# Layer 0 of a decoder: statistics of four chunks together, and gated integers quantised in two halves from a copied scale row

## The chip, the cores and the metric

The kernel runs on one core of a Trainium2 chip. The metric is device time in microseconds, from one launch, lower is better. A core has five engines that run their own instruction queues in order and wait for each other by semaphores: TensorE (PE in the profile; its weight loads are PEld), VectorE (DVE), ScalarE (ACT), GpSimd (POOL) and SyncE (SP, which here only issues DMAs).

## The reference

Two decoder layers over x of 4 batches x 1024 tokens x 256 channels in float32, each layer with self attention, cross attention to a context of 154 tokens, and a feed forward, each followed by x = layernorm(x + f(x)). Layer 0's feed forward is the part that matters most here, a pair of "bit linear" layers with integer activations and ternary weights:

```python
def act_quant(x):
    scale = 127.0 / jnp.clip(jnp.max(jnp.abs(x), axis=-1, keepdims=True), 1e-05)
    return jnp.clip(jnp.round(x * scale), -128, 127) / scale
...
h = bit_linear(x, w1)                 # 256 -> 1024
h = depthwise_conv1d(h.transpose(0, 2, 1), conv_w, conv_b)
h = h.transpose(0, 2, 1)
h = jax.nn.silu(h)
return bit_linear(h, w2)              # 1024 -> 256
```

The gated hidden values (after silu) need one scale per token: 127 over the largest of a token's 1024 absolute values. They are multiplied by it, rounded to integers, and go into the second product. The cross attention of layer 0 has 16 heads of 64, and its output, plus x, is normalised.

## The kernel before, in words

**Tiling.** x lies in SBUF for the whole run, one tile per batch: 128 partitions (tokens) x 8 chunks x 256 channels. Products go through 128 x 128 weight loads and write PSUM banks of 512 floats.

**Stages.** Layer 0's self attention comes first (until about 690 us). Then one list of events holds three things: layer 0's cross attention, layer 0's feed forward, and layer 1's self attention. Feed forward of batches 0 and 1 runs beside cross attention of later batches; feed forward of batches 2 and 3 runs beside layer 1's self attention. Layer 1's cross attention and feed forward close the kernel.

**Order.** Every piece of work is a Python function put into the list with a time in units of its own. `run_in_order` sorts by time (ties keep the order of insertion) and calls them. Instructions on PE, and the last steps of a layernorm, are pinned to that order (`tc.keep_in_program_order`). On the other engines a scheduler orders the instructions beforehand: when an engine is free by its plan, it takes the oldest instruction that is ready, so that work of a later event can run earlier where an engine would stand idle. The feed forward's `schedule` rounds every time before unit 135 down to a whole unit plus 0.42, which places these events in the gaps of the cross attention's own.

**Cross attention, layer 0** (`wide_cross_attention`). A step s is one of 32 (batch, half of the tokens, group of four heads); it takes four units. After each half's last step, `out_projected` (line 775) runs four times, once a chunk: eight products (L574 through the helper `mm`), an add into x (L781) and `measured` (lines 130 to 137), which takes the mean and variance of a chunk with two VectorE instructions, L136 and L137. After the fourth it calls `layernorm`, which forms the reciprocal roots on POOL (L154) and puts the scaling of x (L169) off by six events.

**Feed forward, layer 0** (`feed_forward`). Per batch: `token_scales` (L844), `quantised_x` (a mult L852 and a rounding L858 per half), `token_rows`. Then four rounds r of 256 tokens, in which hidden channels lie on partitions: the tile gt holds 128 x 8 x 256 floats, of which there is one buffer. In a round, `hidden` and `gated` run four times each (products, convolution L920 and L924, gate L934, largest absolute value L939 to L944). Then:

- `hidden_scales`: two PE transposes of the maxima (L949), a reduce (L951) and the four small instructions of `act_scales` (L833, L835, L836, L838) that give the scale sc and its inverse;
- `quantised_hidden`: two PE transposes (L957) spread sc over all partitions as a row in a PSUM bank, one VectorE product of gt with that row (L961), one rounding to bf16 integers into gq (L964);
- `fed_forward`: sixteen products of gq with the second weight (L574), then x is updated (L976) and normalised.

The times within a round, as shares of the batch's length: `hidden_scales` at u + 16 (15.5 for batches 2 and 3), `quantised_hidden` at u + 18.5, `fed_forward` at u + 23, next round at u + 21. A batch has 38, 38, 39 and 40 units. The tile tagged "xq" (one buffer) is shared by the quantised x and the running maximum am of `gated`.

Of the kernel before, what the change touches and what calls it, by code (L numbers as in the profile page):

```python
# [8 lines left out]
F32 = mybir.dt.float32  # L9
BF16 = mybir.dt.bfloat16  # L10
U8 = mybir.dt.uint8
AF = mybir.ActivationFunctionType
ALU = mybir.AluOpType
# [3 lines left out]
P = 128  # L17
# [8 lines left out]
RND = 12582912.0  # L26
# [3 lines left out]
def decoder_kernel(ctx: ExitStack, tc: tile.TileContext, a: dict, out: bass.AP):  # L30
    nc = tc.nc
# [99 lines left out]
    def measured(b, c):  # L131

        if c % 4 == 0:
            measures[b, c // 4] = small.tile([P, 4, nc.vector.BN_AGGR_DIM], F32, tag="bnmv", name="bnmv", bufs=6)
        st = small.tile([P, nc.vector.BN_STATS_DIM], F32, tag="bnst", name="bnst", bufs=2)
        nc.vector.bn_stats(st, xs[b][:, c, :])  # L136
        nc.vector.bn_aggr(measures[b, c // 4][:, c % 4, :], st)  # L137

    def layernorm(b, c0, n, scalar=False, then=None, wait=6):


        xb = xs[b][:, c0 : c0 + n, :]
        if n == 4:
            mv = measures.pop((b, c0 // 4))
        else:
            st = small.tile([P, 2, nc.vector.BN_STATS_DIM], F32, tag="bnst2", name="bnst2", bufs=2)
            mv = small.tile([P, 2, nc.vector.BN_AGGR_DIM], F32, tag="bnmv2", name="bnmv2", bufs=3)
            for c in range(n):
                nc.vector.bn_stats(st[:, c, :], xb[:, c, :])
                nc.vector.bn_aggr(mv[:, c, :], st[:, c, :])  # L150
        ve = small.tile([P, 4], F32, tag="ve", name="ve", bufs=2)
        nc.vector.tensor_scalar(ve[:, :n], mv[:, :n, 1], EPS, None, ALU.add)  # L152
        rstd = small.tile([P, 4], F32, tag="rstd", name="rstd", bufs=3)
        nc.gpsimd.tensor_tensor(rstd[:, :n], ve[:, :n], neghalf[:, :n], ALU.pow)  # L154

        def last_step():
            pin = tc.keep_in_program_order
            if scalar:
                nmr = small.tile([P, 4], F32, tag="nmr", name="nmr", bufs=2)
                pin(nc.vector.scalar_tensor_tensor(  # L160
                    nmr[:, :n], mv[:, :n, 0], -1.0, rstd[:, :n], ALU.mult, ALU.mult
                ))
            for c in range(n):
                if scalar:
                    pin(nc.scalar.activation(
                        xb[:, c, :], xb[:, c, :], AF.Identity, bias=nmr[:, c : c + 1], scale=rstd[:, c : c + 1]
                    ))
                else:
                    pin(nc.vector.tensor_scalar(  # L169
                        xb[:, c, :], xb[:, c, :], mv[:, c, 0:1], rstd[:, c : c + 1], ALU.subtract, ALU.mult  # L170
                    ))
            if then:
                then()

        pending.append([wait, b, last_step, c0])
# [394 lines left out]
    def pe(ins):  # L570
        tc.keep_in_program_order(ins)

    def mm(o, l, r, start, stop):
        pe(nc.tensor.matmul(o, l, r, start=start, stop=stop))  # L574
# [3 lines left out]
    def at(when, f, *args):  # L578
        events.append((when, len(events), f, args))
# [15 lines left out]
    def wide_cross_attention(wk, wf, slot, bank):  # L595
# [179 lines left out]
        def out_projected(b, qh, k):  # L775
            t = bank()
            c = 4 * qh + k
            for t8 in range(8):
                ot = ots[8 * b + 4 * qh + t8 // 2, t8 % 2]
                mm(t[:, :E], ot[:, k * P : (k + 1) * P], l0x_wo[:, t8, :], t8 == 0, t8 == 7)  # L780
            nc.vector.tensor_tensor(xs[b][:, c, :], t[:, :E], xs[b][:, c, :], ALU.add)  # L781
            measured(b, c)
            if k == 3:
                layernorm(b, 4 * qh, 4)


# [17 lines left out]
        for s in range(8 * NB):  # L804
            for j in range(4):
                at(4 * s + j, scores, s, j)
                at(4 * s + j + 3.4, turned, s, j)
            for i in range(2):
                at(4 * s - 3.4 + 2 * i, queries, s, i)
                at(4 * s + 7.9 + 2 * i, weighted, s, i)  # L810
            if s % 4 == 3:
                for k in range(4):
                    last = s == 8 * NB - 1
                    at(4 * s + (10.7 + k if last else (13.45, 17.45, 21.45, 23.45)[k]), out_projected, s // 8, s // 4 % 2, k)


    def feed_forward(wf, bank):
# [7 lines left out]
        scs, dqs, xqTs, rows, edges, gts, ams, sc2s, dq2s, gqs, ths = ({} for _ in range(11))  # L825
        Q = 4
        N = S // Q
# [123 lines left out]
            nc.vector.tensor_reduce(amax, t[:, :N].rearrange("p (j n) -> p j n", j=2), AX.X, ALU.max)  # L951
            sc2s[b, r], dq2s[b, r] = act_scales(amax, w2m)

        def quantised_hidden(b, r):
            t = bank()
            for j in range(2):
                pe(nc.tensor.transpose(  # L957
                    t[:, j * P : (j + 1) * P], sc2s[b, r][:, j : j + 1].to_broadcast([P, P]), ident
                ))
            g = gts[b, r]  # L960
            nc.vector.tensor_tensor(g, g, t[:, :N].unsqueeze(1).to_broadcast([P, 8, N]), ALU.mult)  # L961

            gqs[b, r] = wf.tile([P, 8, N], BF16, tag="gq", name="gq", bufs=1)
            nc.vector.tensor_scalar(gqs[b, r], g, RND, RND, ALU.add, ALU.subtract)  # L964

        def fed_forward(b, r):
            t = bank()
# [13 lines left out]
        def schedule(b, t0, length, start):  # L981
            def on(share, f, *args):
                when = t0 + length * share / 100.0

                at(int(when) + 0.42 if when < start - 4 else when, f, b, *args)

            inside = t0 + length < start
            on(0, token_scales)
            for q in range(2):
                on(3 + 2 * q, quantised_x, q)  # L990
                on(5.5 + 2 * q, token_rows, q)
            on(9, edge_tokens)
            for r in range(Q):
                u = 11 + 21 * r
                for m in range(4):
                    d = 2.65 if inside else 2.0
                    on(u + d * m, hidden, r, m)
                    on(u + d * (m + 1.5), gated, r, m)
                on(u + (16 if inside else 15.5), hidden_scales, r)
                on(u + 18.5, quantised_hidden, r)  # L1000
                on(u + 23, fed_forward, r)

        return schedule
# [115 lines left out]
    wf = ff_stack.enter_context(tc.tile_pool(name="ffn", bufs=1, side="right", reuse_waits="tile"))  # L1119
# [518 lines left out]
```

## Time and profile before

| | us |
|---|---|
| median of the 3 runs shown | 2301.23 |
| their lowest and highest | 2296.64, 2302.22 |
| the profiled execution: its time | 2297.67 |
| the profiled execution: its span (first to last instruction) | 2295.9 |
| granted TensorE clock, mean over the span | 0.977 |

| busy over the span | us | share |
|---|---|---|
| PE | 2158.2 | 94% |
| DVE | 1495.3 | 65% |
| ACT | 1130.5 | 49% |
| POOL | 507.7 | 22% |

| lines that the change touches | instructions | mean ns |
|---|---|---|
| L136, chunk statistics, 128x256 (whole kernel) | 160 | 420 |
| L137, their combination (whole kernel) | 160 | 174 |
| L957, transposes of the scales | 32 | 285 |
| L961, product of gt and the row, 128x2048 | 16 | 2280 |
| L964, rounding into gq, 128x2048 | 16 | 1228 |

How to read it: a row of instructions has the line, the engine, the operation, the tiles it writes and reads, how often, and busy time. A row of waits has who waited, for whom, and then total us, times and the longest. A timeline row has the start and duration in us, and in brackets the idle time of the engine before it with what ended it. A busy engine is not an engine at its peak, and an average over the span mixes stages with different limits.

### The profile page before, as it was taken

How to read it: one execution, taken by the hardware profiler on the slowest of the kernel's cores; microseconds unless marked ns; L12 is line 12 of the kernel's file. 1: busy time of each engine (PE TensorE's matmuls, PEld its weight loads, DVE VectorE, ACT ScalarE, POOL GpSimd, SP SyncE). 2: the span in 40 equal slices, each digit the busy share in tenths (PEclk: the TensorE clock that was granted, in tenths of full speed). 3: DMA queues.
4: the chain of work that ended last, by engine and by line, in shares of the span. 5: the costliest groups of instructions: out<-in, count | busy, mean ns of one | idle time of the engine just before them, and what ended most of it. 6: DMA issues, size and time to landing. Idle time of an engine off the chain costs nothing.

```text
span 2295.9 us, 38089 instructions
## 1 busy us (share of the span) xinstructions
PE 2158.2 (94%) x14196; PEld 1271.0 (55%) x14228; DVE 1495.3 (65%) x3287; ACT 1130.5 (49%) x2925; POOL 507.7 (22%) x1113
## 2 busy tenths in 40 slices
PE   7999999999999899999999998889989999999996
PEld 4444454455444456656556555656666755565554
DVE  4665666667666556557997887785883365555644
ACT  1455555554555365555665655444542334535443
POOL 1111111111112265444444443000000021111102
PEclk8999999999999999999999999999999999999998
DMA  3101110000000100000000000000000010010101
GB/s 89 40 22 33 33 29 15 10 15 15 6 15 1 38 1 19 1 1 1 1 1 1 33 1 22 0 1 1 1 1 1 1 20 15 10 30 14 28 1 37
DMA packets 24440, 34.78 MB, mean 15 GB/s; under 512 B 5952, under 2 KB 19648, under 8 KB 24256
## 3 DMA queue, kind: packets, MB, share of 16 engines
q1 hardware_dynamic: 22640, 31.20, 5.9%
q8 instruction: 113, 1.85, 0.3%
q10 hardware_dynamic: 1616, 1.16, 0.2%
q14 instruction: 71, 0.58, 0.1%
HBM read 15.56 MB, written 4.19 MB: 9 GB/s over the span
## 4 chain that ended last, share of the span: by engine, by line
PE 71%; DVE 19%; ACT 6%; issue 1%; POOL 1%; DMA 1%; SPq 0%; ACTq 0%; POOLq 0%; DVEq 0%
PE s L191 21%; PE t L574 15%; PE s L1174 10%; PE s L574 9%; PE acc L191 6%; DVE gt L924 3%; PE acc L1174 3%; DVE nmp L332 2%; PE t L758 2%; ACT u L733 2%; DVE x L169 1%; DVE nmx L729 1%; DVE bnst L136 1%; PE t L1082 1%; DVE ht L910 1%
## 5 line engine op out<-in xcount | busy, mean ns | idle before, releaser
L398 ACT ACTIVATE p<-s 128x512 f32<-128x512 f32 (+1 forms) x640 | 320.5, 554 | 286.1 <-PE s L191 283.7
L332 DVE TENSOR_REDUCE nmp<-s 128x1 f32<-128x512 f32 (+3 forms) x640 | 298.0, 522 | 154.2 <-PE s L191 153.9
L191 PE MATMUL s<-qs,kp 32*128 32x512 f32 (+3 forms) x1536 | 369.2, 525 | 5.3 <-DVE nmp L332 5.3
L191 PE MATMUL s<-kp,qp 32*128 32x128 f32 (+3 forms) x2304 | 327.5, 408 | 2.1 <-DMA qp<-sq 1.9
L741 POOL TENSOR_SCALAR p<-u,rs 128x128 f32<-128x128 f32 x512 | 214.6, 437 | 294.5 <-DVE rs L737 203.1
L191 PEld LDWEIGHTS s<-kp,qp 32*128 32x128 f32 x2304 | 166.9, 189 | 142.9 <-ACT p L398 45.1
L401 POOL TENSOR_SCALAR_AFFINE_SELECT p<-p 128x256 f32<-128x256 f32 x256 | 101.1, 410 | 640.0 <-ACT p L398 639.7
L733 ACT ACTIVATE u<-s,nmx 128x154 f32<-128x154 f32 x512 | 192.0, 388 | 31.6 <-DVE nmx L729 27.9
L191 PEld LDWEIGHTS s<-qs,kp 32*128 32x128 f32 x1536 | 144.2, 184 | 62.0 <-DVE nmp L332 29.2
L154 POOL TENSOR_TENSOR rstd<-ve,neghalf 128x4 f32<-128x4 f32 (+1 forms) x56 | 55.1, 984 | 545.5 <-DVE ve L152 541.4
L191 PE MATMUL acc<-p,v 128*32 128x512 f32 (+3 forms) x1536 | 159.8, 496 | 1.2 <-ACT ot L440 0.8
L574 PEld LDWEIGHTS s<-kt,qt 64*128 64x128 f32 x1024 | 103.1, 189 | 71.8 <-issue 53.3
L574 PE MATMUL s<-kt,qt 64*128 64x154 f32 x1024 | 137.1, 317 | 0.5 <-ACT qt L715 0.3
L574 PE MATMUL t<-xT,xw 128*128 128x512 f32 x256 | 124.2, 608 | 10.4 <-DVE xT L661 6.6
L729 DVE TENSOR_REDUCE nmx<-s 128x4 f32<-128x616 f32 x128 | 101.2, 791 | 49.9 <-PE s L574 49.7
L1331 DVE TENSOR_REDUCE nmt<-s 128x3 f32<-128x462 f32 (+1 forms) x192 | 99.0, 578 | 45.2 <-PE s L1174 45.1
L924 DVE SCALAR_TENSOR_TENSOR gt<-ht,cw,gt 128x256 f32<-128x256 f32 x256 | 117.5, 498 | 6.6 <-ACT gt L920 5.5
L574 PE MATMUL t<-xw,ot 128*128 128x256 f32 x512 | 116.3, 381 | 3.6 <-ACT pr L762 1.7
L574 PE MATMUL t<-v,pt 128*128 128x256 f32 x512 | 116.2, 380 | 3.1 <-DVE pt L1083 3.1
L574 PE MATMUL s<-qt,xT 128*128 128x512 f32 x256 | 118.4, 606 | 0.0
L348 DVE TENSOR_REDUCE nmp<-s 128x4 f32<-128x512 f32 x128 | 82.5, 687 | 48.6 <-PE s L191 41.3
L574 PEld LDWEIGHTS t<-v,pt 128*128 128x128 f32 x512 | 96.0, 190 | 23.3 <-issue 6.0
(259 smaller groups left out, 3896.2 us busy)
## 6 DMA issues: line engine op xcount, KB each, us to landing
qp<-sq SPq DMA_DIRECT2D x128, 64.0 KB, 2.4
kp<-sk SPq DMA_DIRECT2D x64, 64.0 KB, 2.3
out_dram<-x SPq DMA_DIRECT2D x8, 512.0 KB, 2.9
x<-in_x_dram SPq DMA_DIRECT2D x3, 1024.0 KB, 5.5
wf<-in_L_ffn_w_dram SPq DMA_DIRECT2D x2, 1024.0 KB, 6.0
xw<-in_L_xattn_wk_dram SPq DMA_DIRECT2D x1, 1024.0 KB, 5.2
xw<-in_L_xattn_wq_dram SPq DMA_DIRECT2D x1, 1024.0 KB, 5.7
xw<-in_L_xattn_wv_dram SPq DMA_DIRECT2D x1, 1024.0 KB, 5.2
```

The lines of the kernel that those rows point to most:

```text
L191: pe(nc.tensor.matmul(o, l, r, start=start, stop=stop))
L332: nc.vector.tensor_reduce(nmp[:, 2 * pair + g, qc, i : i + 1], t[g][:, c0 : c0 + n], AX.X, ALU.max)
L348: nc.vector.tensor_reduce(nmp[:, 2 * pair + g, q0 : q0 + 4, 0], t[g].rearrange("p (j n) -> p j n", j=4), AX.X, ALU.max,)
L398: nc.scalar.activation(p[:, g, :total], t[g][:, :total], AF.Exp)
L401: nc.gpsimd.affine_select(out=v, in_=v, compare_op=ALU.is_ge, fill=0.0, base=0, pattern=[[0, 2], [1, P]], channel_multiplier=-1,)
L574: pe(nc.tensor.matmul(o, l, r, start=start, stop=stop))
L729: nc.vector.tensor_reduce(nmx.rearrange("p i g -> p g i"), t, AX.X, ALU.max, negate=True)
L733: nc.scalar.activation(u[:, 2 * i + g, :], t[:, g, i, :], AF.Exp, bias=nmx[:, i, g : g + 1], accum_out=ssum[:, i, g : g + 1],)
L741: nc.gpsimd.tensor_scalar(p[:, h * P : (h + 1) * P], u[:, h, :P], rs[:, h : h + 1], 1.0, ALU.mult, ALU.mult)
L924: nc.vector.scalar_tensor_tensor(g, ht[:, i, k : k + N], cw[:, hc, k : k + 1], g, ALU.mult, ALU.add)
L1174: pe(nc.tensor.matmul(o, l, r, start=start, stop=stop))
L1331: nc.vector.tensor_reduce(nmts[s % 2][:, 3 * u : 3 * u + n, g, 17], ts[g][:, : n * LK].rearrange("p (c k) -> p c k", k=LK), AX.X, ALU.max, ...
```

## The change

In cross attention, the statistics of the four chunks of a half are taken together, after the fourth chunk's add. In the feed forward, the transposes that spread sc become an event of their own, `hidden_rows`, at u + 17.2, and ScalarE copies the row from PSUM into an SBUF tile (tag "xq", in the place of am, which is no longer needed by then). `quantised_hidden` runs twice, at u + 18.5 and u + 20, on four of the eight channel blocks each: a product of half of gt with the row in SBUF, and a rounding into half of gq.

```diff
             nc.vector.tensor_tensor(xs[b][:, c, :], t[:, :E], xs[b][:, c, :], ALU.add)
-            measured(b, c)
             if k == 3:
+                for c in range(4 * qh, 4 * qh + 4):
+                    measured(b, c)
                 layernorm(b, 4 * qh, 4)
...
-        def quantised_hidden(b, r):
+        def hidden_rows(b, r):
             t = bank()
             for j in range(2):
                 pe(nc.tensor.transpose(
                     t[:, j * P : (j + 1) * P], sc2s[b, r][:, j : j + 1].to_broadcast([P, P]), ident
                 ))
-            g = gts[b, r]
-            nc.vector.tensor_tensor(g, g, t[:, :N].unsqueeze(1).to_broadcast([P, 8, N]), ALU.mult)
-
-            gqs[b, r] = wf.tile([P, 8, N], BF16, tag="gq", name="gq", bufs=1)
-            nc.vector.tensor_scalar(gqs[b, r], g, RND, RND, ALU.add, ALU.subtract)
+            row = ams[b, r] = wf.tile([P, 2, N], F32, tag="xq", name="row", bufs=1)
+            nc.scalar.copy(row[:, 0, :], t[:, :N])
+
+        def quantised_hidden(b, r, i):
+            if i == 0:
+                gqs[b, r] = wf.tile([P, 8, N], BF16, tag="gq", name="gq", bufs=1)
+            part = slice(4 * i, 4 * i + 4)
+            g = gts[b, r][:, part, :]
+            nc.vector.tensor_tensor(g, g, ams[b, r][:, 0, :].unsqueeze(1).to_broadcast([P, 4, N]), ALU.mult)
+
+            nc.vector.tensor_scalar(gqs[b, r][:, part, :], g, RND, RND, ALU.add, ALU.subtract)
...
                 on(u + (16 if inside else 15.5), hidden_scales, r)
-                on(u + 18.5, quantised_hidden, r)
+                on(u + 17.2, hidden_rows, r)
+                for i in range(2):
+                    on(u + 18.5 + 1.5 * i, quantised_hidden, r, i)
                 on(u + 23, fed_forward, r)
```

## The prediction

> **What bounds the kernel now.** I read the page first, then the busy time by stretch, then who waits for whom around the two places that the change touches, then the timeline of single instances. The page says that TensorE is busy nearly throughout:
>
> ```profile
> span 2295.9 us, 38089 instructions
> PE 2158.2 (94%) x14196; PEld 1271.0 (55%) x14228; DVE 1495.3 (65%) x3287; ACT 1130.5 (49%) x2925; POOL 507.7 (22%) x1113
> ```
>
> The busy time by stretch (columns: stretch, its length, then PE, PEld, DVE, ACT and POOL busy, granted clock, DMA share, GB/s) separates three situations:
>
> ```profile
> 700.00:1010.00 310.00, 297.14 (x1766) 170.69 (x1766) 175.41 (x398) 163.28 (x606) 126.19 (x318) 0.98 0.04 11
> ...
> 1065.00:1200.00 135.00, 127.99 (x715) 79.82 (x714) 119.79 (x254) 87.50 (x335) 63.34 (x138) 0.98 0.00 1
> 1200.00:1270.00 70.00, 68.88 (x416) 46.59 (x417) 52.54 (x108) 40.35 (x150) 33.99 (x72) 0.99 0.00 1
> 1270.00:1430.00 160.00, 146.23 (x825) 91.21 (x822) 134.17 (x289) 95.18 (x352) 66.66 (x147) 0.96 0.06 20
> 1430.00:1720.00 290.00, 254.96 (x1174) 178.16 (x1172) 223.17 (x489) 139.78 (x287) 11.36 (x13) 0.96 0.00 1
> ```
>
> Until 1010 us cross attention runs alone and is TensorE's. From 1065 to 1430 it is interleaved with the feed forward of batches 0 and 1: PE 343 of 365 us, DVE 307 of 365. From 1430 to 1720 the feed forward of batches 2 and 3 runs beside layer 1's self attention, where both have gaps. The waits of PE show what the feed forward costs it, first for 1065 to 1430, then for 1430 to 1735:
>
> ```profile
> PE t L957 <- DVE sc L836: 4.5, 3, 2.8
> ...
> PE t L574 <- DVE gq L964: 1.8, 1, 1.8
> ```
>
> ```profile
> PE t L949 <- DVE am L944: 12.2, 3, 6.9
> PE t L574 <- DVE gq L964: 8.3, 3, 4.6
> ```
>
> So gq, the product of the edited lines, is waited for, mostly in the later stage. One instance in the timeline (b=1, r=1) shows the order:
>
> ```profile
> 1316.28 0.38 PE L949 MATMUL t<-ident,am 128*128 128x128 f32 x2
> 1316.50 1.88 PE L574 MATMUL t<-xT,xw 128*128 128x512 f32 x4
> ...
> 1317.10 0.41 DVE L951 TENSOR_REDUCE amax<-t 128x2 f32<-128x256 f32 x1
> ...
> 1317.95 0.17 DVE L836 TENSOR_SCALAR sc<-sc 128x2 f32<-128x2 f32 x1
> ...
> 1319.64 0.38 PE L957 MATMUL t<-ident,sc 128*128 128x128 f32 x2
> ...
> 1320.47 2.28 DVE L961 TENSOR_TENSOR gt<-gt,t 128x2048 f32<-128x2048 f32 x1
> ...
> 1323.43 1.36 DVE L964 TENSOR_SCALAR gq<-gt 128x2048 bf16<-128x2048 f32 x1
> ...
> 1324.86 1.92 PE L574 MATMUL t<-L_ffn_w,gq 128*128 128x256 bf16 x16 [1.55 <-ACT u L733]
> ```
>
> Between the transposes of the maxima (L949) and those of the scales (L957) PE has queries, scores and turned probabilities to do, 3 us of them, and the DVE chain reduce, clip, reciprocal, times 127 (L951 to L836, 1317.10 to 1318.12) is over before PE comes back. The wait for gq is 1.55 us here.
>
> **The order after the change.** PE's instructions are pinned to the order of the sorted event times; the other engines' order is a scheduler's. For times before unit 135 the schedule rounds every event to a whole unit plus 0.42. I worked the times out. For the eight instances of batches 0 and 1 (length 38) the shares 16 and 17.2 round to the same unit: 64.42 for (0, 0), 72.42, 80.42, 88.42, 102.42, 110.42, 118.42 and 126.42. So hidden_rows stands directly behind hidden_scales in PE's queue, with nothing between. The shares 18.5 and 20 round to the next unit together, so the two halves stand side by side there too. For batches 2 and 3 (not rounded) hidden_rows is adjacent in (2, 0), (2, 1) and (3, 2); in (2, 2) and (2, 3) it now goes ahead of a weighted sum, or of a score block and a query block; in (3, 0), (3, 1) and (3, 3) a weighted sum still stands between.
>
> **Cost 1: PE waits for the scales, batches 0 and 1.** Where DVE is free, the chain ends 1.45 us after L949's transposes (0.43 until the reduce starts, 1.02 through it), and PE goes on 0.14 later (the distance from L836's end to L957 where PE was waiting). Everything in PE's queue behind it (queries, scores, turned) waits as well, and so do ACT's exponentials. Chain ends after L949 in today's trace, plus 0.14: 1.6, 1.6, 2.2, 1.4, 4.0, 1.6, 6.4 and 2.9 us, together 21.8. In the fifth and seventh a score maximum (0.78) and a probability copy (0.67) ran ahead of the reduce or in its way; both come from PE work that would now be behind, so 2.9 goes. What PE waits there already goes too: 4.5 for sc, and 3.4 for gq (1.55 above, 1.83 before the product at 1409.56), since the mult can start no later than now while PE comes later. 21.8 - 2.9 - 4.5 - 3.4 = 11.0. Bounds: 0 (all given back by later waits) to 17.3 (only the sc waits go). PE's other waits in this stretch are 15 us of 365, so little can be given back; I take 1. Result +10.0.
>
> **Cost 2: clock.** The granted clock halves after pauses. From 1405.9 to 1409.3 PE was busy for 1.82 of 3.40 us (a pause of 1.6) and the next row by stretch, 1409.3 to 1412.7, has 0.50; after the pause of 2.8 at 1359.6 it was 0.50 from 1361.5 to 1371.8. After the 1.55 at 1323.3 nothing fell. Half clock for 3.4 us costs 1.7 of PE's work. Bounds: none to eight (13.6). I take two more stretches, and the one at 1409 fewer: +1.7. [...]
>
> **Cost 3: DVE, ACT, POOL.** Today an instance takes L961 2.28 + L964 1.23 = 3.51 on DVE. Two halves by the rows of the same shape (xr, L852, 128x1024 from SBUF, 1.22; xq, L858, 0.73) take 3.90, 0.39 more, with gaps 0.45, 16 times: 7 us, beside 58 idle us of DVE in 1065 to 1430 and 67 in 1430 to 1720; between 0 and 7, I take 0 in the first and count it by instance in the second. The copy to SBUF lies on ACT between pr (128x128, 267 ns) and ot (128x512, 586 ns): 0.37, and frees the PSUM bank that L961 holds for 2.3 us. ACT is busy 61%; the copy's cost is the 0.6 us (with 0.2 of handover) by which the mult starts later, and what queues behind it on ACT is idle anyway while PE waits. The mult now reads two operands in SBUF. In the trace four GpSimd products took 3.44 us instead of 1.41 from 1407.55 on, while L964 and L852 ran, whereas one beside L961 took its normal 0.36. So 2.4 us of POOL per instance, at most; p lies finished for 2.4 us at the least and some 8 us in the median before PE turns it, so I take 0. [...]
>
> **Gain and loss, batches 2 and 3.** (2, 0): DVE took a 2.29 us filler (amax L844 at 1457.16) because the rows came late; the mult can now go before it: -2.3 of PE's 4.57 us for gq. (2, 1): PE waits 2.1 more at the scales, and loses a 0.6 wait for gq: +1.5. (2, 2): rows 3.5 us earlier, and PE waited 3.58 for gq: -3.5. (2, 3): rows 6 us earlier, but PE had no gap: 0. (3, 0) and (3, 3): the mult 0.6 and its end 1.0 later with a 0.2 to 0.6 us wait already there; the first four products can start on the first half: +0.6 each. (3, 1), (3, 2): 5 and 8 us to spare, 0. Sum -3.1; bounds -9 (half-clock stretches at 1463.9 and 1532.2 go too) and +3 (the scheduler still puts a filler ahead).
>
> **The statistics.** 24 of 32 chunk statistics (0.42 + 0.18 us of DVE) move behind the fourth chunk's add. No work is added. Those who waited for a statistic in 700 to 1450 lost 4 us together; the burst of 2.4 us stands before the scale and shift, which is put off by six events anyway, so the cover is that delay. Between -4 and +4; I take 0.
>
> **Sum.** +10.0 + 1.7 + 0 - 3.1 + 0 = +8.6. The profiled execution took 2297.67 us (span 2295.9, 1.8 around it) and would take 2306; it lies 3.6 below the median of the runs shown, 2301.23, so the forecast is 2310.
>
> **Rivals.**
> *Given back* (0.20): the waits of cost 1 stand before stretches where PE waits for ACT and DVE, and the mult fills DVE meanwhile. Chain steps on gt (L924, 9% of the chain from 900 to 1700) speak for it, 94% PE against. 0 to 2 instead of 10: 2301, within 2295 to 2306.
> *Faster* (0.17), the other side: in 1430 to 1720 the loop scales, mult, quantise, next hidden block, maximum is the bound; L961 lies on the chain of waits there five times, 2.2 us each, and each mult starts as soon as the scales exist. Today it starts 28 us after the scales ended, summed over eight instances; less 1.05 each (copy and longer halves) that is 20. With the pauses the half-clock stretches go: 0.96 of the clock over 290 us is 12 lost, of which up to 10. So -30 in place of -3.1: 2283. It decides from about -19 on, where the time falls under 2294. PE's queue, in which a weighted sum still stands first three times, speaks against.
> *Slower by more* (0.08): every pause halves the clock, or the scheduler puts fillers between reduce and scales, as it did with L844 (2.27 us at 1358.89): +12 on top, 2322.
> *It does not do what it says*: the two halves are neighbours in program order in batches 0 and 1, and split nothing unless an older instruction becomes ready; that is within the forecast.
>
> **How the numbers follow.** The forecast case has 0.55 and its own range 2304 to 2318; some seven tenths of it are over 2308.1, that is over 0.3%, which is about what a measurement here can tell from no change. Slower: 0.41 + 0.08 = 0.49. Same: 0.14 + 0.20 = 0.34. Faster: 0.17. The range 2293 to 2322 leaves out about half of the third rival's and of the second's far ends.
>
> **What would show it.** Right: PE waits for sc eight times at the transposes of hidden_rows, 1.4 to 3 us each, in the stretch of batches 0 and 1; waits for gq there vanish; the mults take 1.22 and the conversions 0.73. Wrong: those waits under 1 us, because PE was late anyway; stretches of the same length as before; p waited for by PE; waits for am L944 in batches 2 and 3 that shrink by more than 5 us.

## The result, and the profile after

The changed kernel took 2308.8 us in the median of six runs (2308.51 to 2309.63), beside 2300.59 us for the kernel before (six runs, 2296.64 to 2302.22). The ratio is 1.0039 with a 95% interval from 1.0029 to 1.0049: slower by 0.4%. The forecast was 2310 us, with 0.49 on slower by over 0.3%. The profiled execution took 2308.68 us, 11.0 us more than the profiled one before. The first lines of the page of the kernel after:

```profile
span 2307.0 us, 38172 instructions
PE 2165.3 (94%) x14228; PEld 1269.7 (55%) x14228; DVE 1499.8 (65%) x3319; ACT 1138.9 (49%) x2941; POOL 516.0 (22%) x1113
```

PE's share is still 94%, so the page alone does not show where the time went. The same stretches as before, of the kernel after (stretch, its length, then PE, PEld, DVE, ACT and POOL busy with the number of instructions, granted clock, DMA share, GB/s):

```profile
700.00:1010.00 310.00, 297.09 (x1769) 171.44 (x1768) 176.97 (x402) 164.33 (x612) 127.68 (x320) 0.98 0.04 11
1065.00:1200.00 135.00, 123.77 (x682) 76.02 (x678) 113.99 (x249) 83.87 (x317) 64.08 (x130) 0.97 0.00 1
1200.00:1270.00 70.00, 67.20 (x391) 45.23 (x392) 49.39 (x99) 36.95 (x138) 32.61 (x69) 0.92 0.00 1
1270.00:1430.00 160.00, 141.05 (x779) 87.95 (x778) 137.12 (x298) 98.55 (x369) 70.14 (x152) 0.95 0.07 20
1430.00:1720.00 290.00, 261.07 (x1238) 182.34 (x1237) 221.06 (x504) 141.26 (x291) 12.84 (x15) 0.97 0.00 1
```

Until 1010 us nothing differs: the same matmuls within three, the same clock. From 1065 to 1430, where the feed forward of batches 0 and 1 is interleaved with cross attention, PE was busy 343 us and is now busy 332; it got through 1852 matmuls instead of 1956, and the clock fell (0.99 to 0.92 in the middle row). From 1430 to 1720 it is the other way round: 261 us instead of 255, and 1238 matmuls instead of 1174. So the change seems to lose in one stage and to win in the next; the two kernels do not do quite the same work in these windows, and the cut by work further down settles it. Who waited, for PE in 1065 to 1440 (a wait, total us, times, longest) in the kernel after:

```profile
PE t L958 <- ACT u L733: 10.7, 5, 4.1
PE t L958 <- DVE sc L836: 5.9, 1, 5.9
...
PE t L958 <- DVE rs L737: 2.3, 1, 2.3
...
PE t L958 <- DVE sc L837: 1.6, 1, 1.6
...
PE t L574 <- DVE gq L971: 0.9, 1, 0.9
```

L958 are the transposes of the scales in `hidden_rows`. PE waits there eight times out of eight, 20.5 us together. Only two rows name sc. The others name an exponential (L733) or the reciprocal of a sum of attention (L737) that happened to come last by the records; what the transposes read is sc of L837. The timeline of one instance (b=1, r=0; start, duration) shows this, and the case in which the reduce comes late:

```profile
1282.72 0.38 PE L950 MATMUL t<-ident,am 128*128 128x128 f32 x2
...
1283.27 1.53 DVE L169 TENSOR_SCALAR x<-x,bnmv,rstd 128x256 f32<-128x256 f32 x4
...
1284.72 0.78 DVE L729 TENSOR_REDUCE nmx<-s 128x4 f32<-128x616 f32 x1
...
1285.42 0.68 DVE L759 COPY pt<-t 128x512 f32<-128x512 f32 x1
...
1286.02 0.41 DVE L952 TENSOR_REDUCE amax<-t 128x2 f32<-128x256 f32 x1
...
1286.87 0.17 DVE L837 TENSOR_SCALAR sc<-sc 128x2 f32<-128x2 f32 x1
...
1287.18 0.66 PE L958 MATMUL t<-ident,sc 128*128 128x128 f32 x2 [4.08 <-ACT u L733]
...
1287.57 3.94 POOL L741 TENSOR_SCALAR p<-u,rs 128x128 f32<-128x128 f32 x4 [2.21 <-DVE rs L737]
...
1287.64 3.04 PE L574 MATMUL t<-xT,xw 128*128 128x512 f32 x4
...
1287.88 0.37 ACT L962 COPY row<-t 128x256 f32<-128x256 f32 x1 [0.69 <-PE t L958]
...
1288.29 2.46 DVE L969 TENSOR_TENSOR gt<-gt,row 128x1024 f32<-128x1024 f32 x2 [0.89 <-ACT row L962]
```

PE finishes the maxima's transposes at 1283.10 and does nothing until 1287.18, then the queries take 3.04 us instead of 1.88 (instance (1, 1) before, shown in the prediction), where the clock is granted at 0.50 from 1286.55 to 1289.96. Both things that cost time in this change are in these lines: the pause, and the half clock behind it. The two products of L969 ran back to back, and POOL's four products beside them took 3.94 us instead of 1.41. For the later stage, PE's waits in 1440 to 1745 of the kernel after:

```profile
PE t L950 <- DVE am L945: 14.7, 4, 6.3
...
PE t L958 <- DVE sc L837: 5.2, 4, 2.1
...
PE t L574 <- DVE gq L971: 0.4, 1, 0.4
```

Before, PE waited 8.3 us for gq here; all but 0.4 of that is gone, and the waits for sc (2.1 before) and am (12.2) grew by 5.6 together.

**Where the 11 us are.** Cut at the same four pieces of work in both traces, the run divides into: the start to the first turned probabilities of cross attention, 808.1 us before and 805.3 after; from there to the maxima of batch 2 (cross attention with the feed forward of batches 0 and 1, called the cross stretch below), 646.3 and 664.1; from there to the last score maximum of layer 1's self attention (the middle stretch, feed forward of batches 2 and 3), 379.0 and 375.3; the rest, 462.5 and 462.2. So -2.8, +17.8, -3.7, -0.3. Of the first, 2.4 arise in the first 80 us of the run, ahead of any changed code. The sum of half-clock time in the cross stretch rose from 27.3 to 44.4 us, in the middle one it stayed at 20.5. The cross stretch in the view by stretch, of the kernel before and of the kernel after, one fence each:

```profile
808.12:1454.39 646.27, 616.48 (x3483) 390.01 (x3481) 477.43 (x1010) 384.23 (x1475) 294.37 (x680) 0.98 0.02 7
```

```profile
805.30:1469.45 664.15, 622.64 (x3482) 391.89 (x3481) 480.48 (x1026) 388.71 (x1483) 302.25 (x680) 0.97 0.02 7
```

The length less PE's busy time is what PE stood idle: 29.8 us before, 41.5 after, 11.7 more. The same PE work also kept it busy for 6.2 us longer, and 17.1 us more of the stretch were at half clock. These two, the pauses and the slower work, make the 17.8 us but for rounding.

**How kernels are compared below.** The program before was run 80 times beside the kernels of this study, on three chips, and took from 2284.25 to 2307.82 us. Its time goes almost exactly with the mean clock granted to PE (0.971 to 0.984): a straight line through the 80 runs falls by 1.78 us per 0.001 of clock, has 2296.3 us at 0.977, and leaves a residual of 0.7 us. The ratios below are estimates with their intervals and not the quotients of the two medians; where the kernel before ran at two clocks (experiments 9 to 12) the two differ most. So for each kernel I give its time and its ratio, its distance from this line at its own clock (mean over its runs; standard errors 0.1 to 0.4), and the stretches of its trace. The distance says what a kernel costs apart from the clock; what it costs through the clock it leaves out. That other kernels follow the slope of the kernel before is an assumption, so kernels whose clocks lie far apart are compared less surely than the standard errors say. The kernel after lies 7.3 us above the line at a clock of 0.974; by the line, 0.003 less clock than in the profiled run before is another 5.3.

### The profile page after: what moved, and what is told of

Read it like the earlier page. It is cut to its first block, busy times and chain, and to the rows that moved or that the text cites. A ratio compares the mean times of both kernels' runs of the same rounds, so it can differ in the third digit from the quotient of the medians.

```text
span 2307.0 us, 38172 instructions
## 1 busy us (share of the span) xinstructions
PE 2165.3 (94%) x14228; PEld 1269.7 (55%) x14228; DVE 1499.8 (65%) x3319; ACT 1138.9 (49%) x2941; POOL 516.0 (22%) x1113
## 4 chain that ended last, share of the span: by engine, by line
PE 70%; DVE 20%; ACT 6%; issue 1%; POOL 1%; DMA 1%; SPq 0%; ACTq 0%; POOLq 0%; DVEq 0%
PE s L191 21%; PE t L574 15%; PE s L1183 10%; PE s L574 8%; PE acc L191 6%; DVE gt L925 4%; PE acc L1183 3%; ACT u L733 2%; DVE nmp L332 2%; PE t L758 2%; DVE x L169 1%; DVE nmx L729 1%; DVE bnst L136 1%; DVE ht L911 1%; DVE am L943 1%
## 5 line engine op out<-in xcount | busy, mean ns | idle before, releaser
L741 POOL TENSOR_SCALAR p<-u,rs 128x128 f32<-128x128 f32 x512 | 221.1, 450 | 305.1 <-DVE rs L737 207.1
L733 ACT ACTIVATE u<-s,nmx 128x154 f32<-128x154 f32 x512 | 192.7, 390 | 31.4 <-DVE nmx L729 30.2
L574 PE MATMUL t<-xT,xw 128*128 128x512 f32 x256 | 131.8, 640 | 9.5 <-DVE xT L661 7.4
L729 DVE TENSOR_REDUCE nmx<-s 128x4 f32<-128x616 f32 x128 | 101.4, 792 | 51.4 <-PE s L574 51.3
```

The lines of the kernel that those rows point to most:

```text
L729: nc.vector.tensor_reduce(nmx.rearrange("p i g -> p g i"), t, AX.X, ALU.max, negate=True)
L733: nc.scalar.activation(u[:, 2 * i + g, :], t[:, g, i, :], AF.Exp, bias=nmx[:, i, g : g + 1], accum_out=ssum[:, i, g : g + 1],)
L741: nc.gpsimd.tensor_scalar(p[:, h * P : (h + 1) * P], u[:, h, :P], rs[:, h : h + 1], 1.0, ALU.mult, ALU.mult)
```

## The experiments

**1. The statistics alone** (the kernel before with the first part of the change).

```diff
             nc.vector.tensor_tensor(xs[b][:, c, :], t[:, :E], xs[b][:, c, :], ALU.add)
-            measured(b, c)
             if k == 3:
+                for c in range(4 * qh, 4 * qh + 4):
+                    measured(b, c)
                 layernorm(b, 4 * qh, 4)
```

> The kernel before with only the statistics of four chunks put together. Theory A (the loss is PE's wait behind the scale chain in batches 0 and 1, the statistics cost nothing): 2297 to 2303, ratio 0.998 to 1.002. Rival S (the burst of eight statistics instructions late in a half is what costs): 2305 to 2309, nearly the whole loss.

Measured: 2295.14 us beside 2303.55 before (0.996, 0.9947 to 0.9973). This looks like a gain, but none shows at equal clock: the distance from the line is +0.3, its stretches after the start are 645.8, 379.0 and 462.6 us against 646.3, 379.0 and 462.5, and its half-clock time in them is the same to a tenth. Its five runs had a mean clock of 0.978 to 0.980, the fifteen of the kernel before on this chip 0.972 to 0.977. So the difference is there and repeats, but it is the clock's, and not in the stretches that hold the edit: taken from 805 us on, the two traces are alike. What gives this kernel the higher clock is open, and so is whether the edit has a part in that. By the stretches and at equal clock, the statistics cost nothing.

**2. The halves alone** (the change without that part).

```diff
             nc.vector.tensor_tensor(xs[b][:, c, :], t[:, :E], xs[b][:, c, :], ALU.add)
+            measured(b, c)
             if k == 3:
-                for c in range(4 * qh, 4 * qh + 4):
-                    measured(b, c)
                 layernorm(b, 4 * qh, 4)
```

> The changed kernel with the statistics back after each chunk. Theory A: 2307 to 2311, the loss stays. Rival S: 2299 to 2303.

Measured: 2308.54 us beside 2303.55 (1.0024, 1.0015 to 1.0034), +7.0 from the line; the kernel after has +7.3. The cross stretch is 661.2, the middle one 375.0 us. The whole effect is the feed forward's.

**3 and 4. The rows later**: everywhere (the third experiment), or in batches 0 and 1 only (the fourth), so that `hidden_rows` falls to the unit of `quantised_hidden`, where the transposes stood before. Copy and halves stay.

```diff
-                on(u + 17.2, hidden_rows, r)
+                on(u + 18.5, hidden_rows, r)
...
-                on(u + 17.2, hidden_rows, r)
+                on(u + (18.5 if inside else 17.2), hidden_rows, r)
```

> The changed kernel with the spreading of the scales back at u + 18.5 in all batches; copy to SBUF and halves stay. Theory A: the eight waits of 1.5 to 6 us in batches 0 and 1 and the half-clock stretches behind them go (-14 to -20), the gain in batches 2 and 3 goes as well (+4 to +7): 2295 to 2303. Rival C (the product from SBUF shuts GpSimd out and the halves lengthen DVE, and that is the loss): 2306 to 2311.

> The changed kernel with the spreading of the scales at u + 18.5 in batches 0 and 1 only, at u + 17.2 in batches 2 and 3. Theory A: the waits go and the gain of batches 2 and 3 stays: 2290 to 2297, 3 to 7 us under the kernel with all rows later, and faster than the kernel before. Rival C: 2305 to 2310.

Measured: 2296.77 us (0.9971, 0.9959 to 0.9982) and 2292.57 us (0.9947, 0.9933 to 0.996) beside 2303.55; -1.8 and -5.3 from the line. The busy time in 1065 to 1430 by the same view, of the kernel after, of the third and of the fourth experiment, one fence each:

```profile
1065.00:1430.00 365.00, 332.01 (x1848) 209.20 (x1845) 300.50 (x644) 219.37 (x823) 166.82 (x350) 0.95 0.03 9
```

```profile
1065.00:1430.00 365.00, 344.12 (x1950) 219.94 (x1949) 305.97 (x664) 223.35 (x833) 165.27 (x348) 0.97 0.03 9
```

```profile
1065.00:1430.00 365.00, 344.10 (x1952) 219.90 (x1950) 306.14 (x664) 223.33 (x832) 165.30 (x348) 0.97 0.03 9
```

PE is back at 344 us and 0.97, and the cross stretch at 646.0 and 645.9 us. The place of the transposes alone owns the loss; copy, halves and POOL's slower products stay in both kernels and cost nothing there. Between the two, the earlier rows in batches 2 and 3 are worth 3.5 us by the line. Experiment 4 is faster than both kernels.

**5. The kernel before again**, as an ordinary run in the next series.

> The kernel before, once more, as a measure of what no change gives. The kernel with the statistics alone came out 8 us faster, though its trace runs 3 us ahead of the first trace of before from the first 60 us on and gains nothing after that. If that is the start of the program (theory start): this run's median lies within 2 us of the other runs of before, ratio 0.999 to 1.001, and its trace differs from the first one only ahead of 100 us, by up to 6 us. If the statistics are worth 8 us: the two traces agree within 1 us everywhere.

Measured: 2304.74 us beside 2304.54 (0.9999, 0.999 to 1.0008). Its trace agrees with the first one within 0.4 us from the start of the cross stretch to its end; then its middle stretch takes 386.4 instead of 379.0 us and its rest 465.3 instead of 462.5, with 17 and 10 us more of half clock. The stretch from 1430 to 1720 of this run (the prediction shows that of the first trace, at a clock of 0.96):

```profile
1430.00:1720.00 290.00, 256.96 (x1161) 180.12 (x1160) 219.28 (x483) 136.84 (x281) 11.44 (x13) 0.94 0.00 1
```

More busy time and 13 matmuls fewer: the same program at a lower clock. A difference of 4 us in this stretch can't be put down to an edit when the clocks of the two traces differ.

**6. The pause filled**: the kernel after with products that nobody reads in front of the scales' transposes, sized to the pauses of the trace. This adds dead work and leaves the result as it is.

```diff
             t = bank()
+            if b < 2:
+                for _ in range({(1, 0): 18, (1, 2): 26}.get((b, r), 7)):
+                    mm(t, ident_bf, w2q[:, 0:2, :].rearrange("p c n -> p (c n)"), True, True)
             for j in range(2):
```

> The changed kernel with 7 (18 and 26 in two rounds with long pauses) products of the second weight with an identity ahead of the spreading of the scales in batches 0 and 1; their result is overwritten. PE then works through the pause. Theory A with the clock as a part: the half-clock stretches of 3.4 us behind the pauses go (some 17 us at half clock more than before, 8 us of work), 2299 to 2303. Theory A without the clock: the pauses themselves are all of it, 2307 to 2311, or more where the products outlast a pause.

Measured: 2302.78 us beside 2304.54 (0.9995, 0.9987 to 1.0004), +9.4 from the line at a clock of 0.978. In 1065 to 1430 of its trace:

```profile
1065.00:1430.00 365.00, 348.45 (x1977) 218.72 (x1974) 304.47 (x654) 221.27 (x827) 168.14 (x351) 0.98 0.03 9
```

The clock rises from 0.95 to 0.98, half-clock time in the cross stretch falls from 44.4 to 20.5 us, and the stretch from 664.1 to 655.8. So about 8 us came back when the clock was kept up, although PE still passes the same time without useful work. What is left, 9.5 us, is not the price of the pause alone: the filled kernel has less half clock than even the kernel before (27.3). By the rows of the cross stretch above, the pause is 11.7 and the slower work 6.2. By the line, the filled kernel gains nothing (+9.4 against +7.3): what it gains, it gains through the clock.

**7. The pause alone**: the kernel before with the transposes moved behind `hidden_scales` in batches 0 and 1; no copy, no halves (the row stays in PSUM, the product is whole).

```diff
-        def quantised_hidden(b, r):
-            t = bank()
+        def hidden_rows(b, r):
+            t = ams[b, r] = bank()
...
+        def quantised_hidden(b, r):
+            t = ams[b, r]
...
+                on(u + (17.2 if inside else 18.5), hidden_rows, r)
                 on(u + 18.5, quantised_hidden, r)
```

> The kernel before with one edit: in batches 0 and 1 the transposes that spread the scales stand right behind those of the maxima, as in the changed kernel. Row in PSUM, product whole, statistics as before. Theory A: +16 to +21 us (2317 to 2322), the whole loss of the changed kernel in that stretch and no gain in batches 2 and 3. Rival C (copy, halves and the product from SBUF carry a good part of the loss): +5 to +10 us.

Measured: 2300.03 us beside 2304.54 (0.998, 0.9971 to 0.9989). The total missed the expectation, and by the raw ratio the pause would be a gain. The trace says otherwise: the cross stretch took 660.1 us, 13.8 more than before, with 37.5 us of half clock, PE stood idle for 41.1 us of it (618.98 busy; 41.5 idle in the kernel after), and its waits there are those of the kernel after:

```profile
PE t L957 <- ACT u L733: 10.5, 5, 4.0
PE t L957 <- DVE sc L835: 5.9, 1, 5.9
...
PE t L957 <- DVE rs L737: 2.1, 1, 2.1
...
PE t L957 <- DVE sc L836: 1.3, 1, 1.3
```

The middle stretch and the rest then ran with 13.7 and 20.1 us of half clock (20.5 and 26.5 before), and are 3.9 and 3.0 us shorter although nothing in them was changed. Its eleven runs had a clock of 0.979 to 0.981, all 27 of the kernel before on this chip 0.971 to 0.974, and the distance from the line is +8.3. So the pause costs what it should where it stands, and something else gave more than that back. Why this kernel is granted the higher clock is open: one explanation is that all later work stands elsewhere against the grid of 3.413 us on which the clock changes in the traces (below), which no run tested.

**8. The new rows in batches 2 and 3 alone**, batches 0 and 1 as before; statistics together. The diff is against the kernel before, and `whole_hidden` is what `quantised_hidden` was there.

```diff
...
-                on(u + 18.5, quantised_hidden, r)
+                if inside:
+                    on(u + 18.5, whole_hidden, r)
+                else:
+                    on(u + 17.2, hidden_rows, r)
+                    for i in range(2):
+                        on(u + 18.5 + 1.5 * i, quantised_hidden, r, i)
```

> Batches 0 and 1 quantise as in the kernel before, batches 2 and 3 as in the changed kernel, statistics of four chunks together. Theory A: the gain of batches 2 and 3 alone, -5 to -8 us against before from 800 us on, 2290 to 2297, up to 3 us under the kernel with rows later in batches 0 and 1 alone, whose halves cost 2.4 us there.

Measured: 2292.12 us beside 2304.54 (0.9944, 0.9932 to 0.9957), -4.1 from the line; the cross stretch is 645.8, the middle one 376.1 us. This is the gain part of the change without its loss part.

**9. The rows behind the queries**: the kernel after with `hidden_rows` in batches 0 and 1 three quarters into its unit, so that the queries of the step stand between the maxima and the scales in PE's queue.

```diff
-                on(u + 17.2, hidden_rows, r)
+                if inside:
+                    at(int(t0 + length * (u + 17.2) / 100.0) + 0.75, hidden_rows, b, r)
+                else:
+                    on(u + 17.2, hidden_rows, r)
```

> The changed kernel with the spreading of the scales one place later in PE's queue in batches 0 and 1: behind the block of queries (1.9 us of PE), at the unit plus 0.75. Theory A, by the trace's stretches: the stretch from the first turned probabilities at 800 us to the maxima of batch 2 shrinks from 664 to 648 to 653 us (1.5 us chains are covered by the queries, those of 4 and 6 us in part, the last one has no queries ahead); the whole 2293 to 2300. Rival C (copy, halves and product from SBUF at the earlier time cost by themselves): 659 to 664 and 2304 to 2309.

Measured: 2292.75 us beside 2299.8 (0.9989, 0.9964 to 1.0014), -0.3 from the line; cross stretch 647.8 us with 23.9 us of half clock. Its waits at the transposes, by the view above:

```profile
PE t L958 <- DVE sc L836: 3.8, 1, 3.8
PE t L958 <- ACT u L733: 3.2, 2, 1.6
PE t L574 <- DVE gq L971: 2.8, 3, 1.5
```

Four products of the queries (1.88 us at full clock) are longer than the chain where DVE is free (1.46 us): four instances don't wait at all and one waits 0.3 us. Two wait 1.6 and 3.8 us because their reduce comes 2.9 and 2.5 us late, and the last, at 1405.38, waits 1.6 because no query is left to stand between. The stretch is back within 1.5 us of 646.3; by the line some 5 us of experiment 4 are still missing, of which these waits and the gq ones are a part.

**10. Filled in batches 2 and 3**: experiment 8 with dead products ahead of the maxima's transposes, where PE waits for am. This too is added work without use.

```diff
             t = bank()
+            for _ in range({(2, 1): 18, (2, 2): 27, (2, 3): 7, (3, 3): 9}.get((b, r), 0)):
+                mm(t, ident_bf, w2q[:, 0:2, :].rearrange("p c n -> p (c n)"), True, True)
             for j in range(2):
```

> The kernel with the early spreading in batches 2 and 3 alone, and products whose result is overwritten (18, 27, 7 and 9 of them, 0.21 us each) ahead of the transposes of the maxima in the four rounds where PE pauses for 4.3, 6.3, 1.8 and 2.4 us. Theory clock (pauses cost a second time through the half clock that follows): half-clock time in batches 2 and 3's stretch falls from 20.5 to under 10 us, the stretch from 376 to 369 to 372, the whole 2284 to 2289. Rival (the stretch is bound by VectorE's chain, the clock there does not matter): 375 to 377 and 2290 to 2295.

Measured: 2289.14 us beside 2299.8 (0.9973, 0.9951 to 0.9994), -4.9 from the line. From 1454 to 1835, experiment 8 and then this one:

```profile
1454.00:1835.00 381.00, 349.64 (x1560) 243.69 (x1559) 249.84 (x550) 162.84 (x322) 16.08 (x21) 0.97 0.00 1
```

```profile
1454.00:1835.00 381.00, 361.75 (x1641) 248.73 (x1643) 254.18 (x565) 164.36 (x325) 17.54 (x23) 0.99 0.00 1
```

The middle stretch went from 376.1 to 370.8 us and its half-clock time from 20.5 to 6.8. The edit takes nothing out of the chain that PE waits for there; what changed is the clock. The rest of this run had 37.8 us of half clock instead of 30.4 and gave 2.4 us back.

**11. Early in batches 2 and 3 with the whole product** (the kernel before with the transposes at u + 17.2 there, row in PSUM, no copy, no halves; the functions are those of experiment 7).

```diff
...
+                on(u + (18.5 if inside else 17.2), hidden_rows, r)
                 on(u + 18.5, quantised_hidden, r)
```

> The kernel before with the spreading of the scales at u + 17.2 in batches 2 and 3, row left in PSUM, product whole, statistics as before. If the gain there is the earlier spreading: the stretch of batches 2 and 3 is 374 to 378 as with halves. If it is the halves: 379 to 386 as in the kernel before.

Measured: 2292.0 us beside 2299.8 (0.9994, 0.997 to 1.0017), -4.1 from the line, the same as experiment 8. The middle stretch of its trace, 380.3 us, tells nothing, since it had 34.1 us of half clock. By the line, the earlier rows own the gain and the halves add nothing to it, although PE still waits 3.2 us for gq here and 0.4 with halves.

**12. The whole product from the copy in batches 0 and 1**: the kernel after, not cut in halves there. The last argument is the number of channel blocks.

```diff
...
-                for i in range(2):
-                    on(u + 18.5 + 1.5 * i, quantised_hidden, r, i)
+                for i in range(1 if inside else 2):
+                    on(u + 18.5 + 1.5 * i, quantised_hidden, r, i, 8 if inside else 4)
```

> The changed kernel with the product and the rounding whole (not in halves) in batches 0 and 1; the copied row, the early spreading and everything in batches 2 and 3 stay. All 71 runs of before so far lie on a line of time against mean granted clock (1.78 us per 0.001, 2296.3 at 0.977, 0.7 us scatter); against that line the changed kernel lies 7.3 us higher, the pause alone 8.3 higher, the early spreading in batches 2 and 3 alone 4.1 lower, so 3 us of the change's loss are without an owner. If the halves own them: 3 to 5 us over the line. If the copy and the product from SBUF (GpSimd shut out) own them: 6 to 8 us over it.

Measured: 2307.39 us beside 2290.61 (1.0068, 1.0041 to 1.0095), +7.0 from the line, cross stretch 660.9 us. It was to settle what is left over: pause (+8.3, experiment 7) and early rows later on (-4.1, experiment 8) make +4.2, and the kernel after has +7.3. The 3 us are not the halves'. In the cross stretch the copy and the operand in SBUF leave little room: PE stood idle there for 41.5 us here (619.38 busy) and in the kernel after, and for 41.1 with the pause alone. A dependence of the two stages on each other remains, and so does the line itself, since the pause alone and the kernel after lie 0.006 apart in clock; no run separates them.

## Why the prediction was right, and where it was off

**Cost 1 (PE waits for the scales, +10.0): right in place and size, wrong in one term.** The queue order worked out from the rounded times was right: the transposes stand directly behind `hidden_scales`, eight times of eight, and moving only them (experiments 3, 4, 9) takes the loss away, while moving only them to this place brings most of it (experiment 7). PE's waits are 1.83, 1.62, 2.34, 1.61, 4.08, 1.60, 5.92 and 1.60 us, 20.6 together, where the prediction had 21.8 less 2.9. The first number was near, though the eighth wait came out 1.6 and not 2.9; the correction of 2.9 failed. It took the score maximum and the probability copy in front of two reduces for results of PE work that would now stand behind the pause. The timeline above shows both still there (L729 and L759, 1284.72 to 1286.10): their PE work lies ahead of the maxima's transposes in the queue, DVE got to it late because of the scale and shift of L169, and the reduce again started 2.92 us late (2.86 before). What was subtracted as already paid held: all of the 4.5 for sc, and 2.5 of the 3.4 for gq (0.9 of a gq wait is left). PE's other waits gave back 1.9, where 1 was taken. In sum PE's idle time in the cross stretch rose by 11.7 us, where the term had +10.0.

**Cost 2 (clock, +1.7): right kind, mis-sized.** Two more half-clock stretches and one fewer were assumed. The cross stretch has 17.1 us more of half clock, which is the length of five such stretches, and the same work kept PE busy for 6.2 us longer. That is 4.5 over the term, the largest miss of the sum, though inside its stated bounds of none to eight stretches. Filling the pauses (experiment 6) took 23.9 us of half clock and 8.3 us of time away. The three rows below, of the kernel before, are what it was sized from (the stretch before the pause, with the pause, and behind it):

```profile
1402.49:1405.90 3.41, 1.90 (x11) 0.71 (x9) 2.76 (x8) 2.40 (x14) 1.73 (x5) 1.00 0.01 2
1405.90:1409.31 3.41, 1.82 (x9) 0.82 (x7) 3.14 (x4) 0.85 (x2) 1.76 (x3) 1.00 0.01 2
1409.31:1412.72 3.41, 3.17 (x15) 2.24 (x16) 3.31 (x4) 0.00 (x0) 2.44 (x3) 0.50 0.03 7
```

PE is busy for 1.90 and 1.82 us in the first two rows, yet only after the second does the clock halve. In these traces half clock followed some pauses of about 1.6 us and not others; with eight pauses, two was too few to take as the middle. In the trace after, the clock halved after the pauses of 1.60 us that end at 1330.93 and 1419.07, and not after those of 1.83 and 1.62 us that end at 1070.00 and 1118.60.

**Cost 3 (DVE, ACT, POOL: nothing): right.** The copy took 0.372 to 0.374 us (0.37 estimated), the products 1.223 in the median (1.22), the roundings 0.686 (0.73). POOL's four products stretched from 1.41 to 3.94 us beside two DVE products with both operands in SBUF, 2.53 more (2.4 estimated as the most), and no wait of PE followed: experiments 3 and 4 keep all of this and their cross stretches, 646.0 and 645.9 us, are that of the kernel before (646.3).

**Batches 2 and 3 (-3.1): right in sum.** -3.7 by the two traces, -4.1 by the line (experiments 8 and 11). In the first instance, for which -2.3 was taken, the product starts 2.27 us after the maxima's transposes instead of 4.59, and PE's wait of 4.57 us for gq is gone. In the second, the prediction had PE wait 2.1 us more at the scales; it waits 1.1 there, and 4.26 at the maxima, where it did not wait before and the prediction had no term.

**The statistics (0): right,** +0.3 by the line (experiment 1).

**The rivals.** *Given back* fell: PE's other waits gave back 1.9 us and not all of the pause, and the clock took 6.2 on top. *Faster* (an effect of -30 in the later stage) fell: taking the loss away leaves -4 to -5. Its clock term of "up to 10" had some truth, for experiment 10 gained 5.3 us in that stretch by the clock alone, but only dead work in the pauses did it, not earlier rows. *It does not do what it says* holds in part: by the line the halves do nothing, in batches 0 and 1 (experiment 12) or in 2 and 3 (experiment 11); what acts is where the transposes stand. *Slower by more* (every pause halves the clock) was nearer than its 0.08: the trace had +6.2 us from the clock, about half of the 12 that it asked for. That the total came out 1.2 us from the forecast is partly luck. By the traces the changed stages made +14.1 (17.8 - 3.7), not +8.6; the start was 2.8 us shorter in the trace after, and the 3.6 us that were added to get from the profiled run to the median were not needed again, as the runs of the kernel after all lie within 1.2 us of each other.

## What to carry to other kernels

When an event is put directly behind its producer in an in-order queue, the producer's chain on the other engine becomes a pause (eight of 1.60 to 5.92 us here): look up what stood between them, and leave at least that much work in between (1.9 us of queries covered five instances of eight to within 0.3 us in experiment 9). Price a pause of TensorE twice, for its length and for the clock that the trace shows behind it; in the cross stretch here the two were 11.7 and 6.2 us. And before a difference of half a per cent is believed, put the granted clock of both kernels beside it, and compare the stretches in which the edit lies, cut at the same work in both traces; experiment 1 was faster by 0.4% and experiment 7 by 0.2%, and in neither did the edited stretch gain anything.

The best versions seen are the change with the rows later in batches 0 and 1 (2292.57 us beside 2303.55), the same stages without any change in batches 0 and 1 (2292.12 beside 2304.54), and that with the pauses of the later stage filled (2289.14 beside 2299.8): each faster than the kernel before beside it, and by 4 to 5 us (0.2%) at equal clock.

## What the runs showed of the hardware

**One program, 24 us.** I had expected runs of one program to agree within a few us. The kernel before took 2284.25 to 2307.82 us, and its mean granted clock accounts for all but 0.7 us of it. In the series of experiments 6 and 7 its clock was always 0.971 to 0.974, in that of experiments 9 to 11 it had two clusters, 0.971 to 0.976 and 0.981 to 0.984, on one chip. The traces point at a part of the reason: in those of the kernels before and after, all changes of the granted clock lie a whole number of 3.413 us apart, and the 37.5 us of half clock in experiment 7's cross stretch are eleven times that. The place of this grid against the program's start differs from run to run (its lines lie 3.02, 3.13 and 1.40 us behind a multiple of 3.413 us in the kernel before, the kernel after and experiment 7), so that the same pause falls differently on it. In experiment 5 the same instructions ran with 17 us more of half clock in the middle stretch than in the first trace. But the place on the grid does not decide alone. The pause of 1.60 us ahead of the scales of (1, 1) lies inside one window of the grid in the kernel after and in experiment 7 alike. That window and the next, in the kernel after and then in experiment 7:

```profile
1327.51:1330.92 3.41, 1.82 (x13) 1.21 (x11) 2.27 (x7) 2.36 (x10) 0.92 (x3) 1.00 0.00 0
1330.92:1334.33 3.41, 3.40 (x6) 1.48 (x6) 2.48 (x3) 0.40 (x2) 3.01 (x4) 0.50 0.00 0
```

```profile
1325.77:1329.18 3.41, 1.81 (x10) 1.12 (x9) 2.93 (x9) 1.79 (x9) 0.91 (x3) 1.00 0.00 0
1329.18:1332.59 3.41, 3.41 (x21) 1.51 (x21) 3.38 (x4) 0.95 (x2) 0.83 (x3) 1.00 0.00 0
```

PE was busy for 1.82 and 1.81 us, and only the first was followed by half clock. What decides in such a case is open, and so is what puts the program into one cluster or the other; no run moved the grid.

**Dead work can pay.** Products that nobody reads, put where PE would have waited anyway, made a stretch 8.3 us (experiment 6) and 5.3 us (experiment 10) shorter, with 23.9 and 13.7 us less of half clock there. At equal clock they gained little or nothing (+9.4 against +7.3, and -4.9 against -4.1).
